# Last layer's adapter gathered for each sequence, value loads one sequence further ahead, first cache gathers moved to rounds 16 to 26, second key turn placed ahead of the values

## The chip, the cores and the metric

The kernel runs on one core of one Trainium2 chip. The metric is the device time of the whole program in microseconds (us), as the median of three runs. In the profile PE is the matmul engine, PEld its weight loads, DVE the vector engine, ACT the scalar engine, POOL the GpSimd engine, SP the engine that only issues transfers.

## The reference

There are 64 sequences of 64 tokens with 512 channels. Four layers follow one another, each added to its input; everything is float32.

```python
x = x + einsum('bct,bcd->bdt', x, weights[cond])                    # layer 0
x = x + x @ W_base.T + (((x @ Wt.T) @ A[i].T) @ B_w[i].T) @ Wp.T * sc[i]   # layer 1
# layer 2: 8 query heads, 4 key/value heads of 64; new keys and values are written into a
# paged cache (257 blocks of 16 tokens a sequence), window of 256 positions, softmax, Wo
x = x + attention(x, caches, block_tables, kv_lens)
# layer 3: one of 8 adapters of rank 16 for each sequence
x = x + x @ W.T + ((x @ A[i].T) @ Bm[i].T) * s[i]
```

## The kernel before

The order of all work is written out by hand: the code runs under a manual schedule, so each engine executes its instructions in the order in which the Python code records them. Transfers are issued on three queues: SP's, ACT's and POOL's. POOL's are the indirect gathers and scatters (helpers `gather`, line 63, recorded at L65, and `scatter`, L71). An engine that waits holds up everything behind it on that engine.

**Rounds.** The first part is a loop of 39 rounds (L882). Rounds 0 to 31 each treat one tile of 128 tokens, which is two sequences: layers 0 and 1 (`first_parts`), the new keys and values (`product_kv`, `new_rows`), and their scatter into two small tables in DRAM, `pk` and `pv` (`put_rows`, L831). All scatters to one table follow each other: each waits until the one before has landed. The queries of a tile come 11 tiles later (`product_q`, `norm_q`, `turn_q`), and their multiplication by the inverse norm is on POOL (L248). Rounds 32 to 38 hold queries alone. At round 32 the last scatters are issued, and behind them on POOL `k_patch(0)`, `v_patch(0)` and `v_patch(1)` (L896 to L898), which gather the patched rows for the first sequences. The first gathers from the old cache are at the rounds that L938 to L949 name: `k_load(0)` at 19 and 20, `v_load(0)` and `v_load(1)` at 21 and 23, `k_copy(0)` at 24 to 27, `v_copy` at 25 and 27, `v_load(2)` at 28, `k_load(1)` at 29 and 30.

**Steps.** The second part is a loop of 128 steps (L1117). A step `s` treats one sequence `b` and one pair of key/value heads `gp`; eight steps make a group `q` of four sequences, and `i = s % 8`. In one step PE computes, in this order: `scores(s + 1)` (tile `psc`), the turn of the probabilities `turn_p(s)` (`pp`), the first turn of keys for the next group (`k_turn`, tile `psk`, steps 3 to 7 by the table `turns`, L1114), one of eight parts of the last layers of the group before (`last_parts`), `values(s)` (`po`), and the second turn of keys. DVE and ACT carry the softmax between: `maxima` (L999), `exponentials` (L1009), `shares` (L1016, L1017), `keep_p` (L1032). Both turns of keys write the single bank `psK`, so a turn waits until the copies of the turn before (L183, L184; on ACT for even `o4`, on DVE for odd) have emptied it; `scores` of a new group wait for the copies of the last turn.

**Values.** For each sequence POOL gathers four times 92 rows (`v_load`, into two buffers `vs_mem`), ACT copies them (`v_copy`, L197, into four buffers `vt_mem`), POOL gathers the patched rows over them (`v_patch`), and three transfers on SP's queue spread 28 of the rows (`v_share`, L208). In the pair of steps of sequence `b` the kernel issues `v_load(b + 3)`, `v_copy(b + 2)`, `v_patch(b + 2)` and `v_share(b + 1)`. Keys go the same way once a group: `k_load` (two gathers), `k_copy` (four copies), `k_patch`, then eight turns.

**The last layers.** `last_parts(q)` (L1051) gives eight parts. The first four multiply by `Wo` (`pso`, L1059). The fifth computes the ranks for all eight adapters at once: `a3_sb` holds 8 x 16 = 128 rows, four matmuls of 128 output rows by 256 columns (`psxa`, L1067), and the product with `mask3` (L1070) leaves each sequence its own adapter, scaled. Then come eight matmuls of 512 columns for `x @ W.T` (`psy`, L1078 and L1084) and two with `bm_sb` (L1086). `mask3` is made in round 19 by `adapters` (L438), the two adapter matrices are loaded in round 9 on ACT's queue (L406, L407).

Of the kernel before, what the change touches and what calls it, by code (L numbers as in the profile page):

```python
# [10 lines left out]
F32 = mybir.dt.float32  # L11
I32 = mybir.dt.int32
AF = mybir.ActivationFunctionType
ALU = mybir.AluOpType
# [4 lines left out]
P = 128  # L19
# [31 lines left out]
def kernel(  # L51
# [41 lines left out]
    def ctile(shape, dt, name, pool=const):  # L93
        return pool.tile(shape, dt, name=name, tag=name)
# [16 lines left out]
    a3_sb = ctile([P, KC, P], F32, "a3_sb")  # L111
    bm_sb = ctile([P, D], F32, "bm_sb")
    iod = ctile([P, 3, 4, 28], F32, "iod")
    ion = ctile([P, 3, 4, 28], F32, "ion")
    mask3 = ctile([P, B], F32, "mask3")
    cen = ctile([P, B], F32, "cen")
    edge = ctile([P, 1], F32, "edge")
    lowb = ctile([P, B], F32, "lowb")
# [175 lines left out]
    with ExitStack() as one:  # L294
# [104 lines left out]
        def late_inputs(part):  # L399
            h = slice(part % 2 * 2, part % 2 * 2 + 2)  # L400
            if part < 2:
                S.dma_start(out=woT_sb[:, h], in_=woT[:, h])
            elif part < 4:
                S.dma_start(out=w3_sb[:, h], in_=w3T.rearrange("(c p) o -> p c o", p=P)[:, h])
            else:
                S.dma_start(out=a3_sb, in_=a3T.rearrange("(c p) r -> p c r", p=P))  # L406
                S.dma_start(out=bm_sb, in_=bm3)  # L407

        def positions(part):

# [12 lines left out]
        def rows0():  # L423

            make_identity(nc, ident)
            iota(pcol, [[0, 1]], 0, 1)
            for _, hs in halves():
                iota(tcol[hs], [[0, 1]], 0, 1)
            for bd in bds:
                G.memset(bd, 0.0)  # L430
            condf = t1([P, B], F32, "condf")
            V.tensor_copy(condf, cond_i)
            for h, hs in halves():
                V.tensor_scalar(
                    cidx[hs], condf[hs].rearrange("p (n two) -> p n two", two=2)[:, :, h],
                    float(T), tcol[hs], ALU.mult, ALU.add)

        def adapters(ad_i, scb, e, dst):  # L438

# [442 lines left out]
        for n in range(NLAST):  # L882
            if n % 4 == 0:
                parts = first_parts(n // 4 + 1)
            w_load0(n + 12)
            x2_load(queries(n + 2))
            if 1 <= n <= NTILE:
                new_rows(n - 1)
            if n != NTILE:
                norm_q(queries(n - 1))()  # L890
            lag = 4 if n < 20 else 3 if n < 22 else 2 if n < 24 else 1
            while done["p"] <= min(n - lag, NTILE - 1):
                put_rows(done["p"])
                done["p"] += 1
            if n == NTILE:
                k_patch(0)  # L896
                v_patch(0)
                v_patch(1)  # L898
                norm_q(queries(n - 1))()
            product_q(queries(n), psP)  # L900
            if n % 4:
                x_load0(n + 8)
            if n in (14, 16, 18, 20):
                gather_indices((n - 14) // 2)
            if n < NTILE:
                parts[n % 4]()
            if n % 4 == 0:
                x_load0(n + 8)
            if n == 1:
                written_rows()  # L910
                places()
            if n in (1, 2):
                for o4 in (0, 1):
                    fill_copy(2 * (n - 1) + o4)
            if n == 2:
                fill_store(pv)
            if n >= 2:
# [7 lines left out]
            if 5 <= n < 10:  # L925
                late_inputs(n - 5)
            if 14 <= n < 18:
                positions(n - 14)
            if n == 19:
                adapters(ad3_i, sc3b, 8, mask3)  # L930
                middles()
            if n == 21:
                residual3()
                G.memset(sm_mem, 0.0)
            turn_q(queries(n - 5 if n == NTILE else n - 2 if n != NTILE - 3 else -1), psO)
            if n < NTILE:
                product_kv(n)
# [12 lines left out]


    def pool2(name, bufs):
# [98 lines left out]
    def last_parts(q):  # L1051

        psy, xa, xq, oT = {}, {}, xqs.pop(q), oTs.pop(q)

        def out_product(ec):
            ps = bank(psM, f"pso{q}_{ec}")
            o = ps[:, :256].rearrange("p (b t) -> p b t", t=T)
            for c in range(4):
                PE.matmul(o, lhsT=woT_sb[:, c, ec * P : (ec + 1) * P],  # L1059
                          rhs=oT[:, c // 2, :, c % 2, :],  # L1060
                          start=(c == 0), stop=(c == 3))
            V.tensor_tensor(xq[:, ec], ps[:, :256], xq[:, ec], ALU.add)

        def ranks():
            ps = bank(psM, f"psxa{q}")
            for c in range(KC):
                PE.matmul(ps[:, :256], lhsT=a3_sb[:, c, :], rhs=xq[:, c],  # L1067
                          start=(c == 0), stop=(c == KC - 1))
            xa[0] = mp.tile([P, 4, T], F32, name=f"xa{q}", tag="xa")
            V.tensor_tensor(  # L1070
                xa[0], ps[:, :256].rearrange("p (b t) -> p b t", t=T),
                mask3[:, 4 * q : 4 * q + 4].unsqueeze(2).to_broadcast([P, 4, T]), ALU.mult)

        def y_first(i):
            n = 2 * q + i
            psy[i] = bank(psM, f"psy{n}")
            for c in range(2):
                PE.matmul(psy[i], lhsT=xq[:, c, i * P : (i + 1) * P], rhs=w3_sb[:, c, :],  # L1078
                          start=(c == 0), stop=False)

        def y_rest(i):
            n = 2 * q + i
            for c in range(2, KC):
                PE.matmul(psy[i], lhsT=xq[:, c, i * P : (i + 1) * P], rhs=w3_sb[:, c, :],  # L1084
                          start=False, stop=False)
            PE.matmul(psy[i], lhsT=xa[0].rearrange("p b t -> p (b t)")[:, i * P : (i + 1) * P],  # L1086
                      rhs=bm_sb, start=False, stop=True)
# [29 lines left out]
    for s, (q, b, gp) in enumerate(steps):  # L1117
# [15 lines left out]
        scores(s + 1)  # L1133
        turn_p(s)
        if 0 < s < 16:
# [13 lines left out]
        second()  # L1149
        if gp:  # L1150
            window(b + 2)
        po = values(s)
        if turn2:
            k_turn(q + 1, *turn2)
        keep_o(s, po)
        if gp == 0:
            v_copy(b + 2)
        if i == 0:
            k_copy(q + 1, 3)
        elif i > 4:  # L1160
            k_copy(q + 2, i - 5)
        if i == 7:
            parts += last_parts(q)
    for part in parts:
# [52 lines left out]
```

## Time and profile before

| what | us |
|---|---|
| median of 3 runs (lowest to highest) | 1236.24 (1232.07 to 1236.6) |
| the profiled execution's own time | 1225.52 |
| its span in the trace | 1223.7 |
| POOL, old values: gathers `vs_mem`, 256 | 310.2 |
| POOL, patched values: gathers `vt_mem`, 64 | 80.0 |
| POOL, old keys: gathers `kt`, 32 | 30.6 |
| PE, `pso`, `psxa`, `psy` with `bm_sb` | 123.2, 30.8, 32.7 |

The program starts 1225.52 - 1223.7 = 1.8 us before or after what the trace spans; the rest of the text counts in the trace's time. The fp32 matmuls each leave two rows in the trace, so 64 matmuls of `psxa` are 128 rows. Busy times are unions: where matmuls overlap, the mean length of one is more than its share. "Idle before" names the time in which an engine stood still just ahead of a group, and what ended it. The page cuts the span into 40 slices: the rounds fill slices 1 to 15, steps begin near 480 us, and the last slice is the tail after the last step. Over slices 20 to 39 the busy share of DVE, ACT and POOL is 5 to 7 tenths each, and PE stands at 8 or 9 tenths.

### The profile page before, as it was taken

How to read it: one execution, taken by the hardware profiler on the slowest of the kernel's cores; microseconds unless marked ns; L12 is line 12 of the kernel's file. 1: busy time of each engine (PE TensorE's matmuls, PEld its weight loads, DVE VectorE, ACT ScalarE, POOL GpSimd, SP SyncE). 2: the span in 40 equal slices, each digit the busy share in tenths (PEclk: the TensorE clock that was granted, in tenths of full speed). 3: DMA queues.
4: the chain of work that ended last, by engine and by line, in shares of the span. 5: the costliest groups of instructions: out<-in, count | busy, mean ns of one | idle time of the engine just before them, and what ended most of it. 6: DMA issues, size and time to landing. Idle time of an engine off the chain costs nothing.

```text
span 1223.7 us, 17686 instructions
## 1 busy us (share of the span) xinstructions
PE 1107.0 (90%) x5622; PEld 639.8 (52%) x5622; DVE 753.0 (62%) x2313; ACT 571.2 (47%) x1472; POOL 613.9 (50%) x601
## 2 busy tenths in 40 slices
PE   4998899999999968879989989999999899999998
PEld 4434444444444434446656656555655565665665
DVE  3775346766666755875665655665665665666561
ACT  1332222232233324555655655655665565666651
POOL 3243323332543351887566666656656656656620
PEclk9999899999899988998999999999999999999999
DMA  8375713234331363546546556556555745756420
GB/s 270 123 258 209 241 41 113 74 102 131 111 114 51 108 171 111 157 117 147 129 113 161 130 126 143 147 126 142 147 127 140 167 121 121 161 139 150 99 64 35
DMA packets 129820, 163.20 MB, mean 133 GB/s; under 512 B 58079, under 2 KB 96891, under 8 KB 125545
## 3 DMA queue, kind: packets, MB, share of 16 engines
q0 software_dynamic: 63872, 85.04, 28.5%
q1 hardware_dynamic: 46416, 53.89, 14.5%
q10 hardware_dynamic: 19440, 23.15, 5.6%
q8 instruction: 45, 0.74, 0.3%
q14 instruction: 47, 0.39, 0.1%
HBM read 139.66 MB, written 50.33 MB: 155 GB/s over the span
## 4 chain that ended last, share of the span: by engine, by line
PE 66%; DVE 8%; issue 7%; DMA 6%; POOL 6%; ACT 3%; ACTq 0%; POOLq 0%; DVEq 0%; SPq 0%
PE pso L1059 9%; PE pp L1025 8%; PE po L1041 7%; PE psc L983 7%; PE ps L787 5%; PE psy L1084 5%; PE q L263 5%; PE kv L820 5%; PE psk L175 4%; PE psy L1078 4%; PE psxa L1067 2%; PE psy L1086 2%; DMA pv<-vt_mem,zidx 2%; POOL vs_mem L65 2%; PE ps L789 2%
## 5 line engine op out<-in xcount | busy, mean ns | idle before, releaser
L65 POOL DMA_INDIRECT vs_mem<-in_vblk_dram,iv_old x256 | 310.2, 1212 | 77.4 <-issue 70.5
L1009 ACT ACTIVATE sm_mem<-sm_mem,mn 128x336 f32<-128x336 f32 x256 | 145.6, 574 | 32.5 <-DVE mn L999 26.9
L65 POOL DMA_INDIRECT vt_mem<-pv,iv_new x64 | 80.0, 1250 | 160.2 <-ACT vt_mem L197 84.0
L999 DVE CUSTOM_DVE_ANT_0 sm_mem<-psc,pen 128x336 f32<-128x336 f32 x256 | 119.6, 501 | 43.6 <-PE pp L1025 22.8
L1041 PEld LDWEIGHTS po<-pT,vt_mem 124*64 124x64 f32 x1536 | 84.9, 137 | 87.0 <-ACT sm_mem L1009 49.2
L1041 PE MATMUL po<-pT,vt_mem 124*64 124x128 f32 x1536 | 118.4, 282 | 12.5 <-ACT pT L1032 7.3
L1059 PE MATMUL pso<-oT,woT_sb 128*128 128x256 f32 x512 | 123.2, 385 | 0.0
L263 PE MATMUL q<-wq_sb,x2q 128*128 128x512 f32 x256 | 120.8, 617 | 1.9 <-DMA x2q<-x2d 1.9
L1025 PE MATMUL pp<-ident,sm_mem 128*124 128x128 f32 x768 | 115.5, 283 | 6.8 <-issue 2.9
L1025 PEld LDWEIGHTS pp<-ident,sm_mem 128*124 128x124 f32 x768 | 81.3, 139 | 70.7 <-issue 58.6
L983 PE MATMUL psc<-kT_mem,qs 64*128 64x336 f32 x512 | 108.2, 498 | 10.7 <-DVE kT_mem L184 9.9
L787 PE MATMUL ps<-kT_mem,kT_mem 128*128 128x512 f32 x256 | 116.9, 600 | 0.6 <-PE ps_fill L493 0.6
L820 PE MATMUL kv<-wkv_sb,xr 128*128 128x512 f32 x256 | 115.4, 595 | 0.4 <-ACT va L828 0.4
L1017 DVE TENSOR_SCALAR sm_mem<-sm_mem,rsum 128x336 f32<-128x336 f32 x256 | 107.2, 419 | 9.1
L248 POOL TENSOR_TENSOR q<-q,rsq 128x512 f32<-128x512 f32 x30 | 31.5, 1050 | 139.7 <-DVE rsq L246 109.0
L1059 PEld LDWEIGHTS pso<-oT,woT_sb 128*128 128x128 f32 x512 | 92.5, 192 | 12.6 <-ACT pen L973 2.1
L175 PE MATMUL psk<-ident,k 84*128 84x84 f32 x512 | 63.8, 251 | 22.9 <-ACT kT_mem L184 9.1
L263 PEld LDWEIGHTS q<-wq_sb,x2q 128*128 128x128 f32 x256 | 50.0, 200 | 61.4 <-issue 61.2
L787 PEld LDWEIGHTS ps<-kT_mem,kT_mem 128*128 128x128 f32 x256 | 49.0, 193 | 61.5 <-issue 60.3
L1032 DVE COPY pT<-pp 124x384 f32<-124x384 f32 x128 | 70.8, 553 | 16.4 <-PE pp L1025 6.9
L1032 ACT COPY pT<-pp 124x384 f32<-124x384 f32 x128 | 61.6, 482 | 35.5 <-PE pp L1025 25.0
L820 PEld LDWEIGHTS kv<-wkv_sb,xr 128*128 128x128 f32 x256 | 46.9, 190 | 57.0 <-issue 55.5
(223 smaller groups left out, 1748.5 us busy)
## 6 DMA issues: line engine op xcount, KB each, us to landing
xt<-in_x_dram SPq DMA_DIRECT2D x32, 256.0 KB
x2d<-xr SPq DMA_DIRECT2D x8, 1024.0 KB
x2q<-x2d SPq DMA_DIRECT2D x32, 256.0 KB
qd<-qt ACTq DMA_DIRECT2D x64, 128.0 KB
qs<-qd SPq DMA_DIRECT2D x16, 512.0 KB
xq<-x2d SPq DMA_DIRECT2D x16, 512.0 KB
out_dram<-ys ACTq DMA_DIRECT2D x32, 256.0 KB
vt_mem<-vt_mem SPq DMA_DIRECT2D x192, 28.0 KB
```

Source lines behind the costliest of these rows:

```text
L65: G.indirect_dma_start(out=dst, out_offset=None, in_=src, in_offset=bass.IndirectOffsetOnAxis(ap=idx, axis=0), **more,)
L175: PE.transpose(ps[:, oq, :], k2[:NP, 4 * oq + o4, 2 * gp : 2 * gp + 2].rearrange("p g d -> p (g d)"), ident[:NP, :NP])
L263: PE.matmul(psq[n], lhsT=xt[:, c, :], rhs=wq_sb[:, c, :], start=(c == 0), stop=(c == KC - 1))
L787: PE.matmul(ps, lhsT=wb_sb[:, c, oc * P : (oc + 1) * P], rhs=x1_mem[:, c, :], start=(c == 0), stop=False)
L820: PE.matmul(pskv[n], lhsT=xrs[s][:, c, i * P : (i + 1) * P], rhs=wkv_sb[:, c, :], start=(c == 0), stop=(c == KC - 1))
L983: PE.matmul(pscs[s][g], lhsT=qts[q][gs, gp, b % 4].rearrange("p h t -> p (h t)"), rhs=kT(q, gp)[gs, b % 4].rearrange("p o c i -> p (o c i) ...
L999: V.tensor_tensor_reduce(rows4(sm)[:, :, :, :28], rows4(pscs[s][g]), rows4(pens[b]), SCALE, 3.0e38, ALU.add, ALU.min, mn)
L1009: S.activation(w, w, AF.Exp, bias=mn, scale=-1.0, accum_out=rsum)
L1025: PE.transpose(pp[:NVK, o, :], sms[s][g][0][:, o * P : o * P + NVK], ident)
L1032: (V.tensor_copy if g else S.copy)(pT, pps[s][g][:NVK])
L1041: PE.matmul(po[g * HD : (g + 1) * HD, :], lhsT=vt(b)[:NVK, o, 2 * gp + g], rhs=pTs[s][g][:, o, :], start=(o == 0), stop=(o == 2))
L1059: PE.matmul(o, lhsT=woT_sb[:, c, ec * P : (ec + 1) * P], rhs=oT[:, c // 2, :, c % 2, :], start=(c == 0), stop=(c == 3))
```

## The change

The rank matrix of the last layer is no longer computed for all adapters. Two new tables, `ia3` and `ib3`, name for each sequence the rows of its adapter; `a_load` gathers for one sequence a [128, 16 x 4] piece of A (the DRAM copy is laid out anew for that), `b_load` for four sequences the rows of B. That is five gathers a group on POOL. With them `ranks` has eight matmuls of 32 output rows by 128 columns, at four column places of the array, and the product with B has two matmuls of 64 contraction rows. The four terms of a rank lie on two strips that B's gathered rows repeat. The order of the last four parts changes with it.

The value pipeline is one sequence longer (`v_load(b + 4)`, `v_copy(b + 3)`, `v_patch(b + 3)`), `v_share(b + 1)` and `k_patch` come one step earlier, the last `k_copy` of a group moves from step 0 to step 7 of the group before, the second key turn goes ahead of `values`, and the first gathers move to rounds 16 to 26. The two loads of round 9 are gone. `adapters` is called for layer 1 alone.

```diff
+        def last_adapters():
+            adf = t1([P, B], F32, "adf8")
+            V.tensor_copy(adf, ad3_i)
+            V.tensor_scalar(ia3, adf, float(P), pcol, ALU.mult, ALU.add)
...
+            for e in range(1, 8):
+                V.tensor_scalar(part, adf, float(e), sc3b[:, e : e + 1], ALU.is_equal, ALU.mult)
+                V.tensor_tensor(scl, scl, part, ALU.add)
...
+            V.tensor_reduce(idx, pick, AX.X, ALU.add)
+            V.tensor_scalar(ib3, idx, 16.0, r_f, ALU.mult, ALU.add)
...
                 v_patch(1)
+                v_patch(2)
...
-                adapters(ad3_i, sc3b, 8, mask3)
+                last_adapters()
...
-            if n in (NTILE - 13, NTILE - 12):
-                k_load(0, n - (NTILE - 13))
-            if n in (NTILE - 11, NTILE - 9):
-                v_load((n - (NTILE - 11)) // 2)
-            if n in (NTILE - 7, NTILE - 5):
-                v_copy((n - (NTILE - 7)) // 2)
-            if NTILE - 8 <= n < NTILE - 4:
-                k_copy(0, n - (NTILE - 8))
-            if n in (NTILE - 3, NTILE - 2):
-                k_load(1, n - (NTILE - 3))
-            if n == NTILE - 4:
-                v_load(2)
+            if n in (NTILE - 16, NTILE - 15):
+                k_load(0, n - (NTILE - 16))
+            if n in (NTILE - 12, NTILE - 11, NTILE - 7, NTILE - 6):
+                v_load(n - (NTILE - 12) if n < NTILE - 10 else n - (NTILE - 9))
+            if n in (NTILE - 9, NTILE - 8, NTILE - 4):
+                v_copy(min(n - (NTILE - 9), 2))
+            if NTILE - 13 <= n < NTILE - 9:
+                k_copy(0, n - (NTILE - 13))
+            if n in (NTILE - 9, NTILE - 8):
+                k_load(1, n - (NTILE - 9))
...
         def ranks():
-            ps = bank(psM, f"psxa{q}")
+            ps = bank(psM, f"psxa{q}")[:, :P]
             for c in range(KC):
-                PE.matmul(ps[:, :256], lhsT=a3_sb[:, c, :], rhs=xq[:, c],
-                          start=(c == 0), stop=(c == KC - 1))
+                for i in range(2):
+                    lo = i * 64 + c % 2 * 32
+                    PE.matmul(ps[lo : lo + 32, :],
+                              lhsT=a3_mem[:, 2 * i : 2 * i + 2, :, c].rearrange("p b r -> p (b r)"),
+                              rhs=xq[:, c, i * P : (i + 1) * P], start=(c < 2), stop=(c >= 2))
...
+        def y_ranks():
+            for i, hs in halves():
+                PE.matmul(psy[i], lhsT=xa[0][hs].rearrange("p b t -> p (b t)"), rhs=b3_mem[hs],
+                          start=False, stop=False)
...
-            lambda: (ranks(), y_first(0)), lambda: y_rest(0), lambda: y_first(1), lambda: y_rest(1)]
+            lambda: (ranks(), y_base(0, (0,), start=True)),
+            lambda: (y_base(1, (0,), start=True), y_ranks()),
+            lambda: (y_base(0, (1, 2, 3), stop=True), y_store(0)),
+            lambda: (y_base(1, (1, 2, 3), stop=True), y_store(1))]
+    def a_load(q, i):
+        gather(a3_mem[:, i].rearrange("p r c -> p (r c)"), a3T, ia3[:, 4 * q + i : 4 * q + i + 1])
+    def b_load(q):
+        gather(b3_mem, bm3, ib3[:, q : q + 1])
...
-    for o4 in range(3):
+    for o4 in range(4):
         k_copy(1, o4)
...
+        if i == 0:
+            k_patch(q + 1)
         if gp == 0:
-            v_load(b + 3)
+            v_share(b + 1)
+            v_load(b + 4)
         else:
-            v_share(b + 1)
-            v_patch(b + 2)
-        if i == 1:
-            k_patch(q + 1)
+            v_patch(b + 3)
...
+        if i in (5, 6):
+            a_load(q, 2 * (i - 5))
+            a_load(q, 2 * (i - 5) + 1)
+        if i == 7:
+            b_load(q)
...
-        po = values(s)
         if turn2:
             k_turn(q + 1, *turn2)
+        po = values(s)
         keep_o(s, po)
         if gp == 0:
-            v_copy(b + 2)
-        if i == 0:
-            k_copy(q + 1, 3)
-        elif i > 4:
+            v_copy(b + 3)
+        if i > 4:
             k_copy(q + 2, i - 5)
+        if i == 7:
+            k_copy(q + 2, 3)
```

More of the change, by code (lines that the diff above doesn't have):

```diff
@@ L110 @@
     w3_sb = ctile([P, KC, D], F32, "w3_sb")
-    a3_sb = ctile([P, KC, P], F32, "a3_sb")
-    bm_sb = ctile([P, D], F32, "bm_sb")
+    a3_mem = ctile([P, 4, 16, KC], F32, "a3_mem")
+    b3_mem = ctile([P, D], F32, "b3_mem")
     iod = ctile([P, 3, 4, 28], F32, "iod")
     ion = ctile([P, 3, 4, 28], F32, "ion")
-    mask3 = ctile([P, B], F32, "mask3")
+    mask3 = ctile([P, B // 4, 2], F32, "mask3")
+    ia3 = ctile([P, B], I32, "ia3")
+    ib3 = ctile([P, B // 4], I32, "ib3")
     cen = ctile([P, B], F32, "cen")
@@ L404, in late_inputs @@
                 S.dma_start(out=w3_sb[:, h], in_=w3T.rearrange("(c p) o -> p c o", p=P)[:, h])
-            else:
-                S.dma_start(out=a3_sb, in_=a3T.rearrange("(c p) r -> p c r", p=P))
-                S.dma_start(out=bm_sb, in_=bm3)
         def positions(part):
@@ L436, in rows0 @@
                     float(T), tcol[hs], ALU.mult, ALU.add)
+        def last_adapters():
+            adf = t1([P, B], F32, "adf8")
+            V.tensor_copy(adf, ad3_i)
+            V.tensor_scalar(ia3, adf, float(P), pcol, ALU.mult, ALU.add)
+            seq_i, r_i = t1([P, 1], I32, "seq_i"), t1([P, 1], I32, "r_i")
+            own_s, r_f = t1([P, 2], F32, "own_s"), t1([P, 1], F32, "r_f")
+            V.tensor_copy(seq_i, pcol)
+            V.tensor_scalar(r_i, seq_i, 15, None, ALU.bitwise_and)
+            V.tensor_copy(r_f, r_i)
+            V.tensor_scalar(seq_i, seq_i, 4, 1, ALU.arith_shift_right, ALU.bitwise_and)
+            V.tensor_copy(own_s[:, 1:], seq_i)
+            V.tensor_scalar(own_s[:, :1], own_s[:, 1:], -1.0, 1.0, ALU.mult, ALU.add)
+            scl, part = t1([P, B], F32, "scl8"), t1([P, B], F32, "part8")
+            V.tensor_scalar(scl, adf, 0.0, sc3b[:, :1], ALU.is_equal, ALU.mult)
+            for e in range(1, 8):
+                V.tensor_scalar(part, adf, float(e), sc3b[:, e : e + 1], ALU.is_equal, ALU.mult)
+                V.tensor_tensor(scl, scl, part, ALU.add)
+            pick = part[:, : B // 2].rearrange("p (q s) -> p q s", s=2)
+            for h, hs in halves():
+                own_b = own_s[hs].unsqueeze(1).to_broadcast([HD, B // 4, 2])
+                two = slice(2 * h, 2 * h + 2)
+                V.tensor_tensor(mask3[hs], scl[hs].rearrange("p (q i) -> p q i", i=4)[:, :, two],
+                                own_b, ALU.mult)
+                V.tensor_tensor(pick[hs], adf[hs].rearrange("p (q i) -> p q i", i=4)[:, :, two],
+                                own_b, ALU.mult)
+            idx = scl[:, : B // 4]
+            V.tensor_reduce(idx, pick, AX.X, ALU.add)
+            V.tensor_scalar(ib3, idx, 16.0, r_f, ALU.mult, ALU.add)
         def adapters(ad_i, scb, e, dst):
@@ L924 @@
                 mixers(n // 4 + 2)
-            if 5 <= n < 10:
+            if 5 <= n < 9:
                 late_inputs(n - 5)
@@ L1064, in ranks, with y_base, y_store @@
         def ranks():
-            ps = bank(psM, f"psxa{q}")
+            ps = bank(psM, f"psxa{q}")[:, :P]
             for c in range(KC):
-                PE.matmul(ps[:, :256], lhsT=a3_sb[:, c, :], rhs=xq[:, c],
-                          start=(c == 0), stop=(c == KC - 1))
-            xa[0] = mp.tile([P, 4, T], F32, name=f"xa{q}", tag="xa")
+                for i in range(2):
[3 more added lines that the diff above has]
+                              rhs=xq[:, c, i * P : (i + 1) * P], start=(c < 2), stop=(c >= 2))
+            xa[0] = mp.tile([P, 2, T], F32, name=f"xa{q}", tag="xa")
             V.tensor_tensor(
-                xa[0], ps[:, :256].rearrange("p (b t) -> p b t", t=T),
-                mask3[:, 4 * q : 4 * q + 4].unsqueeze(2).to_broadcast([P, 4, T]), ALU.mult)
-        def y_first(i):
+                xa[0], ps.rearrange("p (b t) -> p b t", t=T),
+                mask3[:, q].unsqueeze(2).to_broadcast([P, 2, T]), ALU.mult)
+        def y_base(i, cs, start=False, stop=False):
             n = 2 * q + i
-            psy[i] = bank(psM, f"psy{n}")
-            for c in range(2):
+            if start:
+                psy[i] = bank(psM, f"psy{n}")
+            for c in cs:
                 PE.matmul(psy[i], lhsT=xq[:, c, i * P : (i + 1) * P], rhs=w3_sb[:, c, :],
-                          start=(c == 0), stop=False)
-        def y_rest(i):
-            n = 2 * q + i
[L1083 to L1087, printed above, removed]
+                          start=start and c == cs[0], stop=stop and c == cs[-1])
+        def y_ranks():
+            for i, hs in halves():
+                PE.matmul(psy[i], lhsT=xa[0][hs].rearrange("p b t -> p (b t)"), rhs=b3_mem[hs],
+                          start=False, stop=False)
+        def y_store(i):
+            n = 2 * q + i
             ys = ap2.tile([P, D], F32, name=f"ys{n}", tag="ys")
@@ L1199 @@
         "w3T": a["L3_cond_W"].T,
-        "a3T": a["L3_cond_A"].reshape(P, D).T,
+        "a3T": a["L3_cond_A"].reshape(8, 16, KC, P).transpose(0, 3, 1, 2).reshape(8 * P, 64),
         "bm3": a["L3_cond_Bm"].transpose(0, 2, 1).reshape(P, D),
```

## The prediction, made before the result

> **What bounds the kernel now.** I read the page's busy shares first, then the chain of work that ended last, then PE's waits in the stretch between two rank products of the chain, then POOL's rows of one period.
>
> ```profile
> span 1223.7 us, 17686 instructions
> PE 1107.0 (90%) x5622; PEld 639.8 (52%) x5622; DVE 753.0 (62%) x2313; ACT 571.2 (47%) x1472; POOL 613.9 (50%) x601
> ```
>
> PE is busy for 90% of the span and nothing else is near it; the chain also lies on PE for 66%. The chain's rows give the length of one group of eight steps:
>
> ```profile
> 620.77 1.76 PE psxa L1067 x8
> ...
> 1144.94 1.77 PE psxa L1067 x8
> ```
>
> The rank product comes once a group. The two rows stand twelve groups apart: (1144.94 - 620.77) / 12 = **43.68 us a period**. The view of windows and PE's waits over exactly this stretch:
>
> ```profile
> 620.77:1144.94 524.17, 486.67 (x3218) 310.43 (x3217) 327.24 (x1104) 318.65 (x852) 325.85 (x276) 1.00 0.58 138
> ```
> ```profile
> PE psc L983 <- DVE kT_mem L184: 8.2, 12, 0.9
> PE psk L175 <- issue: 6.1, 13, 0.9
> PE psk L175 <- PE pp L1025: 5.9, 4, 1.6
> PE psk L175 <- ACT kT_mem L184: 5.5, 6, 1.8
> PE po L1041 <- issue: 4.9, 10, 0.7
> PE po L1041 <- ACT pT L1032: 3.3, 3, 1.2
> ```
>
> The window's first column after the length is PE's busy time, 486.67 / 12 = 40.56 a period, so PE stands still for 3.1. The waits (total, times, longest) say where: before the key turns (`psk`, 6.1 + 5.9 + 5.5 + 0.3 = 17.8, or 1.48 a period), before a new group's scores (`psc`, 0.68 a period), before the values (`po`, 0.68). POOL, the fifth busy column, works 325.85 / 12 = 27.15 a period in 23 gathers, but it cannot issue them back to back:
>
> ```profile
> 564.70 1.22 POOL L65 DMA_INDIRECT vs_mem<-in_vblk_dram,iv_old  x1 [0.30 <-issue]
> 566.22 1.20 POOL L65 DMA_INDIRECT vs_mem<-in_vblk_dram,iv_old  x1 [0.30 <-PE pp L1025]
> ```
>
> Each has 0.30 ahead of it, so POOL's own period is 27.15 + 23 x 0.30 = **34.05**, with 9.6 of slack.
>
> **The change part by part, per period.**
>
> *Ranks.* Removed: four matmuls of 128 output rows by 256 columns, 1.76 (the chain row). Added: eight of 32 output rows by 128 columns. The nearest row is `po` (64 output rows, 128 columns), 12 rows or six matmuls in 0.81 from start to next start (724.14 to 724.94, listed length 0.88): 0.135 each, 8 x 0.135 = 1.08. Gain 0.68. Bounds: 0.54 if strips run twice as much abreast as `po`'s, and 1.76 if a matmul of half the columns costs half of 0.44 and nothing overlaps.
>
> *Product with B.* Removed: two matmuls of 128 rows by 512, 0.86 each, 1.72. Added: two of 64 contraction rows on two halves of the array; nearest is `psc`, two matmuls of 64 rows by 336 in 0.77 (719.85 to 720.62), times 512 / 336 = 1.17. Gain 0.55; bounds 0.86 (fully abreast) and 1.72. Together 1.23, bounds 0 to 2.1.
>
> The rows put a `po` and a `psc` next to full products with no listed gap (690.50 `po`, 691.40 `psc`, 692.16 `pp`). The Trainium skill speaks against the change here: "TensorEngine Tiling (Array Packing)", section Key Properties, says that a change of tiling mode drains the array, and the change adds four such switches a period. With some 128 cycles for a drain, from "TensorE: Matmul & The Clock Gate", section Step-by-step: what each phase is for, an estimate would be 0.2 a period and a median of 1198 rather than the forecast; no row of this trace prices a drain.
>
> *Second key turn ahead of the values.* Its copies get the time of `values` (0.81) before the next user of the bank. The wait of `psc` (0.68, longest 0.9) goes; of the 1.48 before the turns the one of step 6 goes (0.45 at 721.94) and about a third of the rest, together 0.8; a turn (0.44) placed ahead of `po` fills 0.3 of its 0.68. Sum 1.8; bounds 0, since the softmax's loop through DVE and ACT may simply hand the waits to `pp` and `po`, and 2.6 (psc and psk whole, with 0.4 of po). What is late next is `po` on `pT`. PE alone would have 43.68 - 1.23 - 1.8 = 40.65.
>
> *POOL.* Five gathers come in. `a_load` has 128 rows of 256 B, as have the adapter gathers of the rounds:
>
> ```profile
> L65 POOL DMA_INDIRECT wg<-in_w_dram,cidx x32 | 31.8, 992 | 38.1 <-DVE bd L754 27.4 <-issue 5.9 <-DVE cidx L434 3.4
> ```
>
> 5 x (0.99 + 0.30) = 6.45; bounds 5 x 1.25 (`kt`, 0.95) and 5 x 1.55 (`vt_mem`, 1.25): 6.3 to 7.8. POOL's own period becomes **40.5**, as long as PE's. POOL also waits: `v_patch` for ACT's copy or the shares (129.1 / 48 = 2.7 each time, 10.8 a period). These waits are mostly its slack, and shrink when it is late; the extra sequence of lead makes the copy come earlier. A late POOL is felt through ACT, which waits in `v_copy` for `vs_mem` to land, with the probabilities' copies behind it. What is queued behind `a_load` is the next `v_load`; a_load itself waits for the ranks of step 4, which are over before step 5.
>
> Two loops of 40.65 and 40.5 that wait on each other do not both run free. I take back 0.75 of the 1.8, and take **41.4**, bounds 40.5 (POOL's sum) and 43.7. Fourteen periods: 14 x 2.3 = **-32**. Group 15 and the tail have no key turns and few gathers: 2 x 1.23, **-2**.
>
> *End of the rounds.* Here PE's longest wait but one stands, and POOL is its cause:
>
> ```profile
> 435.80 0.99 POOL L65 DMA_INDIRECT kt<-in_kblk_dram,ik_old  x1 [0.31 <-issue]
> 440.63 1.00 POOL L71 DMA_INDIRECT pv<-va,sidx  x1 [3.85 <-DMA pk<-k,sidx]
> ...
> 447.15 0.97 POOL L71 DMA_INDIRECT pv<-va,sidx  x1 [4.22 <-DMA pv<-va,sidx]
> ...
> 452.48 1.03 POOL L65 DMA_INDIRECT k<-pk,ik_new  x1 [3.08 <-DMA pk<-k,sidx]
> ```
> ```profile
> 457.79 1.12 PE L283 MATMUL pst<-ident,q 128*128 128x128 f32 x4 [9.65 <-POOL q L248]
> ```
>
> Four `vs_mem` gathers (422.91 to 428.81) and two `kt` gathers stand between scatters that must land one after another; the patches end at 456.65, and only then comes the multiplication L248 for which PE waits 9.65. With the gathers out of these rounds the scatters keep the pace of rounds without gathers, 3.2 (308.64 to 311.80). The `pv` scatter that goes at 429.12 now can go near 423.5 (the gathers ahead of it take 6.2), three more end its chain at 433.5, the last `pk` lands some 4 after that, near 438.8, and `k_patch` (1.33) and three `v_patch` (one more than before, 1.55 each) end near 444.8; DVE's `rsq` is ready at 443.1. `pst` follows 1.1 after the start of L248, as now, near 446 instead of 457.79: **-11**. Bounds -8 (scatters no faster than 4) and -13.5 (wait 9.65, the 1.87 on `x2q`, and two products at 3.60 instead of 4.62).
>
> *First group, 486 to 548.* POOL is busy 54.05 of 62 there, with the last queries' inverse norms (1.83 + 1.04) between gathers. Five gathers more, 6.45, of which 3.0 is found idle in its steps 5 to 7; `k_patch(1)` now waits for the fourth key copy, near 491.3 where POOL is free at 489.6, +1.6. Less the gain of one early `v_patch`: **+4**, bounds 0 and +8.
>
> *Costed at nothing.* `last_adapters` has 23 more DVE instructions in round 19; DVE is 31.5 busy of the 50 in 250 to 300. Uncovered they cost 23 x 0.2 = 4.6. The fourth `k_copy` (ACT, 1.04) moves from step 0 to 7: ACT is 26.6 busy of 43.7. The moved gathers lie where POOL waits for `rsq` (109.0 in all, 5 to 12 a round); if they push an L248 out they cost PE what they overrun, 1.5 each. `v_share` a step earlier holds SP's queue, with the loads of `xq` and `qs` behind it; SP already waits 375.1 there (57 times, longest 12.9) with PE not waiting for either load. Two loads of 512 KB leave ACT's queue in round 9, where PE's waits are not on them.
>
> Sum: -32 - 2 - 11 + 4 = **-41**. The profiled execution took 1225.52, and the median of the runs is 1236.24, 10.7 above; the differences are worked out in the former and set off from the latter: 1236.2 - 41 = **1195**.
>
> **The rivals.**
> 1. *POOL is no hindrance.* The waits that shrink are all its slack and PE keeps the whole 3.0: period 40.6, 14 x 3.1 = 43; 1236.2 - 43 - 2 - 7 = **1184**. For: the 2.7 before each `vt_mem` is long and ended by ACT, not by data. Against: no slack is left, and each loop that slips then moves the other.
> 2. *POOL binds with some waits on top.* 40.5 + 1.9 (a fifth of 10.8) = 42.4; -18 - 2 - 7: **1209**. For: `v_patch` waits on the landing of other transfers (20.9 of 160.2) that no lead shortens.
> 3. *The waits come back in the softmax, and small tiles do not run abreast.* The period falls by 0.5: -7 - 2 - 7: **1220**, or 1230 to 1242 if the first group costs 8 and the period does not fall. For: PE's `po` waits already end on `pT`. Against: PE had no wait of that kind in 1060 to 1145, where a period is 42.
> 4. *POOL falls behind: slower.* The place is `v_patch(b + 3)` behind the added `a_load` in steps 5 to 7. It decides when the five gathers cost more than (43.68 - 34.05) / 5 = 1.93 each, or bring 3.2 us of new waits a period; then ACT stands in `v_copy` and PE behind it. At a period of 45: +18 - 2 - 7, **1246**. For: a wait inside POOL's queue holds all later gathers. Against: the nearest rows cost 1.25 to 1.55.
>
> That the change does not do what it says is little of a rival: the recorded order on PE does put the second turn before `values`, and five gathers a group are there.
>
> **How the numbers follow.** Forecast (41 to 42) 0.38; rival 1 0.17; rival 2 0.23; rival 3 0.10; rival 4 0.12. The range goes from 1174 (a period at POOL's 40.5, 14 x 3.2 = 44.5, 2 x 2.1 for group 15 and the tail, 13.5 at the end of the rounds, nothing lost in the first group) to 1224 (rival 3); out of it fall half of rival 3, rival 4 and a little below, 0.2. About 0.5%, 6 us, is what can be told from no change: faster is the first three and half of the fourth, 0.83; same is the other half and 0.02 of rival 4, 0.07; slower 0.10.
>
> **What would show it.** Right: `psxa` near 1.1 and the B product near 1.2; no wait of `psc` on `kT_mem`; rank products 41.4 apart; POOL's gathers `a3_mem` x64 and `b3_mem` x16 near 1.0; no wait of 9.65 at `pst` near 446 to 458. Wrong: `vt_mem` or `vs_mem` waits on PE's chain, `v_copy` on ACT waiting for landings, `pp` or `po` waits up by what `psk` lost, or new waits of PE in rounds 16 to 26.

## The result, and the profile after

The changed kernel takes 1311.8 us in the median of four runs (1302.41 to 1327.09), against 1236.42 (1232.07 to 1244.99) for the kernel before in the same series: a ratio of **1.0575, interval 1.0486 to 1.0665**. The forecast was 1195, and the range ended at 1224. The experiments below add something that one number hides: on another chip, where the kernel before takes 1199.9, the ratio of the same two kernels is 0.9993 (0.9957 to 1.0030).

The page of the changed kernel, its first part:

```profile
span 1310.9 us, 18171 instructions
PE 1119.8 (85%) x5750; PEld 637.1 (49%) x5750; DVE 765.6 (58%) x2335; ACT 568.1 (43%) x1472; POOL 693.6 (53%) x680
```

PE has more busy time than before (1119.8 against 1107.0), although its work became less, and a smaller share. The next two rows are rank products thirteen groups apart; the window between them has the columns of the windows shown in the prediction.

```profile
579.05 1.08 PE L1099 MATMUL psxa<-xq,a_mem 128*32 128x128 f32 x11
...
1234.62 0.67 PE L1099 MATMUL psxa<-xq,a_mem 128*32 128x128 f32 x16
```
```profile
579.05:1234.62 655.57, 545.64 (x3589) 339.09 (x3588) 363.63 (x1201) 342.63 (x924) 418.12 (x363) 0.95 0.50 128
```

A period is 655.57 / 13 = 50.43 us where it was 43.68. PE is busy for 41.97 of it (before 40.56) and idle for 8.46 (before 3.1). Thirteen times 6.75 is 88, and the spans differ by 87.2: what comes before and after them about cancels out, and the loss lies in these groups. It has two parts, idle time (+5.4 a period) and matmuls that last longer (+1.4, though the new tiles save some).

**Results are seen late.** PE's waits of this window, and then one stretch of it on three engines:

```profile
PE po L1071 <- issue: 21.8, 34, 4.0
PE po L1071 <- ACT pT L1062: 12.9, 16, 5.8
PE po L1071 <- DVE pT L1062: 12.6, 9, 3.4
PE psk L177 <- ACT kT_mem L186: 11.8, 12, 4.2
```
```profile
710.50 0.83 PE L1013 MATMUL psc<-kT_mem,qs 64*128 64x336 f32 x4
713.06 1.02 PE L1055 MATMUL pp<-ident,sm_mem 128*124 128x128 f32 x6 [1.73 <-PE psc L1013]
713.92 1.89 PE L1089 MATMUL pso<-oT,woT_sb 128*128 128x256 f32 x8
721.57 1.62 PE L1071 MATMUL po<-pT,vt_mem 124*64 124x128 f32 x12 [5.76 <-ACT pT L1062]
```
```profile
713.33 0.56 DVE L1002 SCALAR_TENSOR_TENSOR pen<-ion,lowb,pen 128x336 f32<-128x336 f32 x1
717.80 0.51 DVE L1029 CUSTOM_DVE_ANT_0 sm_mem<-psc,pen 128x336 f32<-128x336 f32 x1 [3.91 <-remote]
```
```profile
717.76 0.27 ACT L1079 COPY oT<-po 128x128 f32<-128x128 f32 x1 [3.25 <-remote]
721.04 0.48 ACT L1062 COPY pT<-pp 124x384 f32<-124x384 f32 x1 [3.02 <-remote]
```

The scores (`psc`) end by the model at 711.33, and DVE, idle since 713.89, begins to read them at 717.80. ACT begins to copy `po`, which was issued at 709.70, at 717.76, and `pp`, which ended by the model at 714.08, at 721.04. Both engines stand still, both are let go within 0.04 us, and then `po` waits 5.76 for ACT. The readers were not slow: the trace records the updates of PE's semaphore at 717.73 and 717.78, 0.02 to 0.03 ahead of both starts. What PE had produced was signalled, and seen, 6 to 7 us after its modelled end. On the other chip the scores of the next step of the same kernel read:

```profile
690.01 0.84 PE L1013 MATMUL psc<-kT_mem,qs 64*128 64x336 f32 x4
```
```profile
690.87 0.51 DVE L1029 CUSTOM_DVE_ANT_0 sm_mem<-psc,pen 128x336 f32<-128x336 f32 x1
```

Modelled end 690.85, semaphore update 690.85, start 690.87; DVE was busy until then. The Trainium skill, "Perfetto Trace Analysis", section Tensor Engine Instruction, says that a matmul's end is computed and that its semaphore is sent only once PSUM has acknowledged the bytes. By that, rows alone cannot tell a late matmul from a late signal: model and start differ by at most 0.02 here on one chip and by 6.5 on another, and which of the two is late no run shows.

**The clock follows.** PE stands from 715.81 to 721.57, and the seventh column of figures in the windows is the granted clock:

```profile
716.00:720.00 4.00, 0.00 (x0) 0.00 (x0) 1.03 (x4) 0.27 (x1) 3.32 (x3) 0.75 0.34 86
720.00:724.00 4.00, 2.43 (x16) 1.73 (x16) 1.97 (x6) 2.34 (x7) 0.00 (x0) 0.50 0.63 180
```

After the wait the clock is 0.50, and the scores at 723.12 take 1.49 instead of 0.83. Over the execution the clock was 0.953 against 0.976 before. The traces' clock records hold 1 and 0.5 alone, so that is 2 x 0.047 x 1310.9 = 123 us at half speed against 59. In the window of thirteen groups it is 70.7 us, in the prediction's window of the kernel before none. PE is busy in 59.2 of the 70.7, so an estimate of what half speed costs is 59.2 / 2 / 13 = 2.3 a period, most of the 1.4 added and the 1.8 that the small tiles save. The Trainium skill, "TensorE: Matmul & The Clock Gate", section What's actually happening, says the same: an idle window of some 3.4 us brings half the clock.

### The profile page after: what moved, and what is told of

Same layout as the page of the kernel before. It is cut to its first block, busy times and chain, and to the rows that moved or that the text cites. A ratio compares the mean times of both kernels' runs of the same rounds, so it can differ in the third digit from the quotient of the medians.

```text
span 1310.9 us, 18171 instructions
## 1 busy us (share of the span) xinstructions
PE 1119.8 (85%) x5750; PEld 637.1 (49%) x5750; DVE 765.6 (58%) x2335; ACT 568.1 (43%) x1472; POOL 693.6 (53%) x680
## 4 chain that ended last, share of the span: by engine, by line
PE 55%; DVE 12%; issue 10%; ACT 7%; POOL 6%; DMA 3%; another core or an unknown queue 3%; ACTq 0%; POOLq 0%; SPq 0%; DVEq 0%
PE po L1071 7%; PE pso L1089 7%; PE ps L818 6%; PE pp L1055 6%; PE kv L851 6%; PE psc L1013 5%; PE q L265 5%; PE psy L1112 5%; PE psk L177 3%; POOL vs_mem L65 3%; PE ps L820 2%; DVE sm_mem L1047 2%; PE psz L803 1%; ACT k L159 1%
## 5 line engine op out<-in xcount | busy, mean ns | idle before, releaser
L1071 PE MATMUL po<-pT,vt_mem 124*64 124x128 f32 x1536 | 133.6, 293 | 54.7 <-issue 24.1
L1029 DVE CUSTOM_DVE_ANT_0 sm_mem<-psc,pen 128x336 f32<-128x336 f32 x256 | 121.7, 503 | 77.6 <-PE pp L1055 34.7
L1055 PE MATMUL pp<-ident,sm_mem 128*124 128x128 f32 x768 | 121.9, 289 | 27.9 <-DVE rsum L1046 7.9
L1071 PEld LDWEIGHTS po<-pT,vt_mem 124*64 124x64 f32 x1536 | 93.4, 142 | 103.2 <-issue 48.6
L1013 PE MATMUL psc<-kT_mem,qs 64*128 64x336 f32 x512 | 114.3, 523 | 18.0 <-DVE kT_mem L186 11.0
L1112 PE MATMUL psy<-w_sb,xq 128*128 128x512 f32 x256 | 127.7, 623 | 0.8 <-issue 0.8
L1089 PE MATMUL pso<-oT,woT_sb 128*128 128x256 f32 x512 | 127.5, 393 | 0.7 <-ACT oT L1079 0.6
L1047 DVE TENSOR_SCALAR sm_mem<-sm_mem,rsum 128x336 f32<-128x336 f32 x256 | 111.3, 435 | 9.0
L1079 ACT COPY oT<-po 128x128 f32<-128x128 f32 x128 | 33.6, 263 | 121.3 <-PE pp L1055 52.8
L177 PEld LDWEIGHTS psk<-ident,k 84*128 84x128 f32 x512 | 52.5, 151 | 65.5 <-issue 33.4
```

The lines of the kernel that those rows point to most:

```text
L177: PE.transpose(ps[:, oq, :], k2[:NP, 4 * oq + o4, 2 * gp : 2 * gp + 2].rearrange("p g d -> p (g d)"), ident[:NP, :NP])
L1013: PE.matmul(pscs[s][g], lhsT=qts[q][gs, gp, b % 4].rearrange("p h t -> p (h t)"), rhs=kT(q, gp)[gs, b % 4].rearrange("p o c i -> p (o c i) ...
L1047: V.tensor_scalar(w, w, rsum, None, ALU.mult)
L1055: PE.transpose(pp[:NVK, o, :], sms[s][g][0][:, o * P : o * P + NVK], ident)
L1071: PE.matmul(po[g * HD : (g + 1) * HD, :], lhsT=vt(b)[:NVK, o, 2 * gp + g], rhs=pTs[s][g][:, o, :], start=(o == 0), stop=(o == 2))
L1089: PE.matmul(o, lhsT=woT_sb[:, c, ec * P : (ec + 1) * P], rhs=oT[:, c // 2, :, c % 2, :], start=(c == 0), stop=(c == 3))
```

## The experiments

For every run the table has the ratio to the kernel before in its own series (intervals in brackets), the period (mean of thirteen, between rank products) and a **delay**. For the delay I paired every maxima L1029 (L999 before) with the scores that it reads, and every L1092 with its `pso`, kept those ahead of which DVE stood idle, after 560 us, and took the start minus the modelled end.

| run | kernel before | ratio | period | mean delay (number over 1 us, of) |
|---|---|---|---|---|
| before, first profile | 1236.4 | | 43.7 | 1.06 (38 of 96) |
| after, first profile | 1236.4 | 1.0575 [1.0486, 1.0665] | 50.4 | 2.13 (87 of 126) |
| c_before | 1233.7 | 1.0018 [0.9979, 1.0056] | 44.4 | 1.21 (44 of 101) |
| c_after | 1233.7 | 1.0486 [1.0415, 1.0557] | 48.6 | 1.88 (109 of 148) |
| e5_group0_adapters | 1233.7 | 1.0249 [1.0152, 1.0345] | 46.9 | 2.16 (101 of 124) |
| e6_old_last_turns | 1233.7 | 1.0439 [1.0348, 1.0529] | 48.5 | 2.03 (99 of 131) |
| h0_group0_adapters | 1238.9 | 1.0151 [1.0089, 1.0213] | 47.0 | 2.12 (111 of 131) |
| h1_no_key_gathers | 1238.9 | 1.0030 [1.0000, 1.0060] | 44.1 | 0.81 (26 of 103) |
| h2_no_value_patches | 1238.9 | 1.0166 [1.0086, 1.0246] | 47.6 | 2.20 (77 of 112) |
| h3_before_no_keys | 1238.9 | 0.9654 [0.9597, 0.9710] | 41.5 | 0.17 (1 of 71) |
| e1_old_last | 1198.6 | 0.9856 [0.9816, 0.9897] | 41.1 | 0.06 (0 of 53) |
| e2_old_turns | 1198.6 | 1.0095 [1.0061, 1.0129] | 42.9 | 0.11 (0 of 61) |
| e3_kpatch_back | 1198.6 | 1.0094 [1.0060, 1.0129] | 43.0 | 0.19 (0 of 81) |
| e4_vpipe_back | 1198.6 | 1.0136 [1.0087, 1.0186] | 43.0 | 0.15 (0 of 72) |
| g0_old_last | 1199.9 | 0.9857 [0.9783, 0.9932] | 41.1 | 0.06 (0 of 53) |
| g1_pipe_only | 1199.9 | 0.9928 [0.9893, 0.9963] | 42.4 | 0.16 (0 of 81) |
| g2_kpatch_only (profile of its longest run) | 1199.9 | 1.0108 [1.0008, 1.0207] | 44.0 | 0.09 (0 of 57) |
| g3_after | 1199.9 | 0.9993 [0.9957, 1.0030] | 42.0 | 0.10 (0 of 60) |
| i1_pipe_only | 1199.4 | 0.9917 [0.9886, 0.9949] | 41.8 | 0.15 (0 of 83) |
| i2_kpatch_only | 1199.4 | 1.0135 [1.0089, 1.0182] | 43.7 | 0.06 (0 of 53) |

By the run records, the series with 1198.6 and 1199.9 ran on chip 1, the one with 1199.4 on chip 8, the one with 1233.7 on chip 5 and the one with 1238.9 on chip 10; for the first comparison no chip is recorded. I call 1 and 8 the quick chips and the others, with that of the first comparison, the slow ones, after the kernel before. Only chip 1 was used in two series, so something else that differs between series, such as where the data lay, is not excluded as the source.

### First series: undo one part at a time (quick chip)

`e1_old_last` takes back `ranks`, the parts of `last_parts`, `adapters` and the loads of round 9; `e2_old_turns` the order of two calls; `e3_kpatch_back` the place of the key patch; `e4_vpipe_back` the pipeline. The copies, loads and patches ahead of the steps that belong to the last two go back as well and are left out here:

```diff
 e2_old_turns
-        if turn2:
-            k_turn(q + 1, *turn2)
         po = values(s)
+        if turn2:
+            k_turn(q + 1, *turn2)
 e3_kpatch_back
-        if i == 0:
-            k_patch(q + 1)
...
             v_patch(b + 3)
+        if i == 1:
+            k_patch(q + 1)
...
+        if i == 0:
+            k_copy(q + 1, 3)
-        if i == 7:
-            k_copy(q + 2, 3)
 e4_vpipe_back
-            v_share(b + 1)
-            v_load(b + 4)
+            v_load(b + 3)
         else:
-            v_patch(b + 3)
+            v_share(b + 1)
+            v_patch(b + 2)
...
-            v_copy(b + 3)
+            v_copy(b + 2)
```

> The changed kernel with the last layers of the kernel before (rank product for all adapters, no gathers of adapters). Theory A, POOL's five added gathers are what costs: about 1230, 80 below the changed kernel. Theory B, key patch at the head of step 0 (62 us of new waits at the head of POOL's queue): no more than 15 below, about 1300. Theory C, second key turn ahead of the values: about 1310. Theory D, the transfers of the longer value pipeline meet those of keys and of the x and q loads: about 1305.

> The changed kernel with the values ahead of the second key turn again. Theory C: about 1235, 75 below the changed kernel. Theories A, B and D: within 15 of 1312.

> The changed kernel with the key patch behind the value patch of step 1 and the fourth key copy in step 0, as before the change. Theory B: about 1240, with the 62 us of waits of the key patch gone from POOL's list. Theory D: some 20 to 40 below 1312, as one part of the traffic moves by a step. Theories A and C: within 15 of 1312.

> The changed kernel with the value pipeline as long as before (loads three ahead, copies and patches two ahead, shares with odd steps). Theory D: about 1240. Theories A, B and C: within 15 of 1312.

The numbers of all four expectations missed: the kernel before itself took 1198.6 here, and the changed kernel had not been run beside them. No theory follows from this series alone; read with `g3_after` (0.9993 on the same chip, another series) it says that each of turns, key patch and pipeline is worth 1.0 to 1.4% to the changed kernel there, and the new last layers cost 1.4%.

### Second series: the changed kernel and the one before, again (slow chip)

> The changed kernel again, beside the others of this series. The kernel before took 1198.6 in the first series of experiments, not 1236. If the chip has no part in the loss: 1.0575 times the kernel before, some 1268. If the loss needs a chip on which the results of the matmuls are seen late (the kernel before at 1236): at most 1.015 times the kernel before.

> The kernel before, for its profile beside the others. Where it takes about 1199: periods of about 42 instead of 43.7, and no starts of DVE and ACT that come 1 to 2 us after the modelled end of the matmul. Where it takes 1236: as in the first profile.

`e5_group0_adapters` gathers for the first group only; `e6_old_last_turns` is `e1_old_last` with the two calls of `e2_old_turns`:

```diff
-        if i in (5, 6):
+        if s in (5, 6):
             a_load(q, 2 * (i - 5))
             a_load(q, 2 * (i - 5) + 1)
-        if i == 7:
+        if s == 7:
             b_load(q)
```

> The changed kernel with adapters gathered for the first group alone; the other groups use the same ones, so that the last layer is that of other adapters from the second group on. 75 of 80 gathers of adapters are left out, the small matmuls stay. Theory A (the five gathers a group are what costs): below the version with the old last layers by 14 to 16 periods of 1.7, so 0.965 of the kernel before. Theory B (key patch at the head of step 0): as the changed kernel.

> The version with the old last layers, and the values ahead of the second key turn again: what is left is the longer value pipeline, the order of POOL and the early gathers. If the second turn ahead of the values is worth 1.8 a period: 25 above the version with the old last layers, 1.007 of the kernel before. If it is worth nothing: as that version, 0.986.

The loss came back on a chip where the kernel before takes 1233.7. Theories A (adapters) and C (turns) fall as its whole cause: `e6_old_last_turns` has neither and still takes 1.0439, with a delay as large as the changed kernel's; both numbers expected for it missed. `e5_group0_adapters` (1.0249) lies between what A and B expected: leaving the adapters' gathers out is worth 0.024 of the 0.049. What is left in `e6_old_last_turns` is the longer value pipeline, the key patch in step 0 and the early gathers.

### Third series: the remaining two parts (quick chip 1 again)

`g1_pipe_only` is `e6_old_last_turns` with the edit of `e3_kpatch_back`, `g2_kpatch_only` with that of `e4_vpipe_back`.

> The version with the old last layers again, whose ratio was 0.986 where the kernel before took 1199. If a chip on which results are seen late turns gains into losses: where the kernel before takes 1230 or more, at or above 1.02; where it takes 1199, 0.986 again.

> Of the change in the steps only the longer value pipeline with the shares a step earlier (key patch behind the value patch of step 1, old turns, old last layers; early gathers as changed). Theory B (key patch at the head of step 0 costs): at most 1.00 of the kernel before, where the version with both was 1.044. Theory D (longer pipeline costs): 1.03 or more there.

> Of the change in the steps only the key patch at the head of step 0 and the fourth key copy in step 7 (value pipeline, turns and last layers as before; early gathers as changed). Theory B: 1.03 or more where the kernel before takes 1230. Theory D: at most 1.00.

> The changed kernel once more. If the loss needs a chip on which results are seen late: at most 1.015 where the kernel before takes 1199, 1.05 where it takes 1230 or more. If the chip has no part in it: 1.05 on either.

This chip shows no delay, in any kernel, and the changed kernel loses nothing, as expected for it. What `g0`, `g1` and `g2` were to tell of a slow chip stays unanswered. The series does show what the changed kernel is bound by when results come in time. POOL first, then PE's and ACT's longest waits, from one rank product to the one thirteen groups on:

```profile
573.01:1119.14 546.13, 505.09 (x3589) 325.92 (x3589) 364.76 (x1196) 341.57 (x923) 423.17 (x367) 0.98 0.69 155
```
```profile
PE po L1071 <- ACT pT L1062: 30.7, 26, 3.0
```
```profile
ACT vt_mem L199 <- DMA vs_mem<-in_vblk_dram,iv_old: 49.7, 12, 5.6
```

POOL works 423.17 / 13 = 32.55 a period in 28 gathers; with 0.30 ahead of each that is 40.95 of 42.01. PE needs only 505.09 / 13 = 38.85. So POOL, with 1.06 to spare, is the nearest bound; ACT stands in `v_copy` until the value rows land, and PE's `po` waits for the probabilities queued behind that copy. Without the new last layers (`g0_old_last`) POOL has slack and PE goes from rank product to rank product in 41.12:

```profile
567.41 1.93 PE L1066 MATMUL psxa<-xq,a_sb 128*128 128x256 f32 x8
...
1102.01 1.93 PE L1066 MATMUL psxa<-xq,a_sb 128*128 128x256 f32 x8
```

It was faster than both kernels on this chip, twice (0.9856 and 0.9857); on a slow chip it was not run.

### Fourth series: which transfers delay the results (slow chip)

`h1_no_key_gathers` and `h3_before_no_keys` have the same edit, on the changed kernel and on the one before; `h2_no_value_patches` patches eight sequences:

```diff
 h1_no_key_gathers, h3_before_no_keys (k_load and k_patch)
-        if q < B // 4:
+        if q < 2:
             gather(...)
 h2_no_value_patches
-        if b < B:
+        if b < 8:
             gather(vt_mem[:NV, b % 4], ...)
```

> The changed kernel with adapters gathered for the first group alone (from the second group on the last layer uses the first group's adapters). Where the kernel before takes 1199 and the changed kernel the same: the small matmuls are worth 14 x 1.6 and POOL has its slack back, so 0.97. If the small matmuls gain nothing: 0.986, as the version with the old last layers.

> The changed kernel without the gathers of old and new keys from the third group on (keys of the groups before are used again). If the packets of 8 and 16 KB that these gathers move make the matmuls' results reach DVE and ACT late where the kernel before takes 1230 or more: the late starts in steps 3 to 5 go, and with them the loss, to 0.96 of the kernel before. If the lateness has another source: no more than the 3 gathers of POOL a group, 1.03. Where the kernel before takes 1199: 0.97, for POOL's 3 x 1.3 a group.

> The changed kernel without the value patches from the ninth sequence on (new values are left out there). POOL has 4 x 1.55 a group less, as if four of the five adapter gathers had gone, and waits for ACT's copies no more. If small packets of the patches make results late: the loss goes. If the keys' packets do: 1.01 to 1.03 where the kernel before takes 1230. Where it takes 1199: 0.965, if POOL's length is what holds the changed kernel there.

> The kernel before without the gathers of keys from the third group on. If these packets make results late in it too: 0.96 where it takes 1236, and 0.99 or more where it takes 1199, as POOL has slack in it.

In the kernel before, leaving out three gathers a group takes the delay from 1.1 or 1.2 to 0.17 and the period to an even 41.5, with a ratio of 0.9654 (0.96 was expected). The window of thirteen groups, and PE's waits in it:

```profile
570.24:1110.13 539.89, 519.72 (x3487) 334.84 (x3485) 356.21 (x1195) 344.64 (x923) 313.90 (x261) 1.00 0.37 99
```
```profile
PE psc L983 <- DVE kT_mem L184: 8.6, 13, 0.7
PE psk L175 <- issue: 7.6, 17, 0.6
PE psk L175 <- ACT kT_mem L184: 3.8, 9, 0.5
```

POOL had 9.6 a period to spare there, and the delay is what changed, so I put the gain down to it: **some 2 us of the 43.7 in the very profile that the prediction was worked out from**. That is argued, as the edit also takes work from POOL; that the same kernel with all its gathers takes 34 to 40 us less on the quick chips points the same way, but it was not profiled there. The changed kernel itself was not run on this chip; set against its other slow series (delay 2.13 and 1.88), the same edit takes its ratio to 1.003 and the delay to 0.81, where 0.96 or 1.03 was expected. 

What remains in `h1_no_key_gathers` sits elsewhere. The trace records the updates of PE's semaphore. I counted, from 560 us to step 118, the matmuls that update it and call one late when no update follows within 0.06 us of its modelled end; in the changed kernel the packets of the key gathers (8 and 16 KB) lie in steps 1 to 4 of a group:

| run | late in steps 1 to 4 | late in the other steps |
|---|---|---|
| before, first profile | 214 of 406 | 93 of 375 |
| h3_before_no_keys | 110 of 394 | 64 of 375 |
| after, first profile | 316 of 416 | 215 of 362 |
| h1_no_key_gathers | 139 of 418 | 263 of 362 |
| g3_after (quick) | 4 of 416 | 1 of 362 |

Without key gathers the lateness falls in the steps where they ran; in the changed kernel it stays in the others, step 6 among them (94 of 98 in the first profile, 72 of 98 in `h1_no_key_gathers`). So the key gathers are not its only source there, and no run tells what else is. Value patches seem to have a part in the time (1.0166 without them, in the range of 1.01 to 1.03 that was expected if the keys' packets do it) and none in the delay (2.20), so their small packets are not the source. `h0_group0_adapters` keeps a delay of 2.12 with hardly any adapter gathered, so these gathers are not its source either; their part in the time (1.0151 and 1.0249 without them, 1.0486 and 1.0575 with) I put down to POOL's queue. The delay alone does not order the runs: `h0_group0_adapters` has 2.12 at 1.0151, `e6_old_last_turns` 2.03 at 1.0439.

### Fifth series: pipeline or key patch (quick chip 8)

> Again the kernel with only the longer value pipeline and the shares a step earlier (and the early gathers); 0.993 where the kernel before takes 1200. Where it takes 1230 or more: 1.03 or above if the value loads that run further ahead meet the key transfers and the x and q loads there and make more results late; 1.00 or below if the key patch in step 0 does.

> Again the kernel with only the key patch at the head of step 0 and the fourth key copy in step 7 (and the early gathers); 1.011 where the kernel before takes 1200. Where it takes 1230 or more: 1.03 or above if the key patch in step 0, beside the x and q loads, makes more results late; 1.00 to 1.01 if the longer pipeline does.

The chip was another one, as quick as the first, so the question was not answered. The ratios repeat those of the third series, near what was expected for such a chip.

## Why the prediction was wrong

**The step that failed** is the reading of the bound: "PE stands still for 3.1. The waits (total, times, longest) say where". It takes PE's work, the order and POOL's sum for all that sets a period, and the sum has no term for results that are seen late. In `h3_before_no_keys`, with the order untouched and the delay nearly gone, PE stands still for (539.89 - 519.72) / 13 = 1.55 a period: the wait of `psc` stays (0.66 against 0.68), that before the turns goes from 1.48 to 0.88, that before `po` (0.68) is no longer listed. So about half of the 3.1 was order and half was not. Two things follow:
- On the quick chip the period of the changed kernel was nearly the forecast one (42.0 against 41.4), but the kernel before takes 1199.9 there instead of 1236.4, and nothing is won.
- On slow chips, with results as late as shown, it was 50.4 and 48.6. With the delay down to 0.81 it was 44.1 (`h1_no_key_gathers`).

The delay is 1.9 to 2.2 in every slow-chip run with the longer value pipeline, the moved key patch and its key gathers, against 1.1 to 1.2 in the kernel before. Why the change makes it longer no run shows; that it packs transfers more closely is a guess.

**Rival 4** had the sign ("POOL falls behind: slower") and neither the mechanism nor the price: POOL's gathers cost what the rows said, and a period was 50.4, not 45. One of its conditions did hold, at a place that I had costed for the first group alone. `k_patch` at the head of step 0 waits for the fourth key copy: it starts 0.30 after the end of that copy in each of these groups (704.13 after 703.83), whatever releaser a row names. POOL's waits in the window of the changed kernel:

```profile
POOL k L65 <- PE pso L1089: 47.1, 11, 7.9
...
POOL k L65 <- DVE pT L1062: 7.3, 1, 7.3
...
POOL k L65 <- ACT k L159: 6.0, 1, 6.0
```

That is 60.4 / 13 = 4.6 a period, where the kernel before shows 0.30 each time. It is not shown to be a loss of its own: POOL's work with 0.30 ahead of each gather is 418.12 / 13 + 28 x 0.30 = 40.6 of the 50.4 here, and on the quick chip the same waits are 8.3 / 13 = 0.6. On the quick chips the key patch alone costs 1.1 and 1.4% (`g2_kpatch_only`, `i2_kpatch_only`), and in the company of the other parts it gains 1.0% (`e3_kpatch_back` is slower without it); what it does on a slow chip was not told apart.

**The other terms, one by one:**
- *Small tiles:* right, and better than forecast. From start to next start the ranks take 0.60 (forecast 1.08) and the product with B 1.06 (1.17), together 1.8 saved where 1.23 was put and 2.1 was the bound. The two rows that show it:

```profile
730.96 0.68 PE L1099 MATMUL psxa<-xq,a_mem 128*32 128x128 f32 x16
731.56 0.70 PE L1112 MATMUL psy<-w_sb,xq 128*128 128x512 f32 x1
```
```profile
737.08 1.13 PE L1118 MATMUL psy<-b_mem,xa 64*128 64x512 f32 x4
738.14 0.51 PE L177 MATMUL psk<-ident,k 84*128 84x84 f32 x4
```

  The switches of tiling, which the prediction priced at an estimated 0.2 a period, show no gap: nothing is listed ahead of the next product. As PE's ends are modelled, a price inside the 0.60 and the 1.06 is not excluded.
- *POOL:* right as a sum, on the chip where nothing else disturbs it: 40.95 against 40.5, and a period of 42.0 against 41.4. There the five gathers cost more than the small tiles win: the last layers as a whole are a loss of 1.4%.
- *Turns:* worth 1% to the changed kernel on the quick chip (1.0095 without), 42.9 - 42.0 = 0.9 a period where 1.8 was put, or 1.05 after the 0.75 taken back.
- *End of the rounds:* the wait of 9.65 is gone, PE is busy 17.85 of 20 in 440 to 460 instead of 8.48, and the first values start at 489.39 instead of 490.76 (483.93 and 491.68 in the second series). Between the matmul below and the first values the changed kernel gains 7.0, and 10.1 in the second series, where 11 was put. Ahead of it 5.0 is lost, for which the prediction had the price (4.6) but costed it at nothing, the 23 added DVE instructions of round 19:

```profile
313.06 2.07 PE L794 MATMUL ps<-bd,xt 128*128 128x128 f32 x8 [7.42 <-ACT kT_mem L796]
```
```profile
307.45 2.07 PE L763 MATMUL ps<-bd,xt 128*128 128x128 f32 x8 [2.38 <-ACT kT_mem L765]
```

  The second row is the kernel before. Without these instructions and with the early gathers the wait is 2.38 too (`g0_old_last`).
- *First group:* +3.7 (489.39 to 579.05 against 490.76 to 576.7), +1.3 in the second series; forecast +4.
- *The clock:* not in the sum at all. Idle stretches of several us cost twice, as PE runs at half speed after them (0.50 after the 5.76 shown).

**What stays open:** what on the slow chips makes results late, beyond the part that goes with the key gathers, and why the quick chips are free of it; and whether the longer pipeline, the key patch in step 0 or the early gathers lengthen the delay.

## What to carry to other kernels

Before waits are costed as order, compare the start of a reader that stood idle with the end of the matmul it reads: where that gap is 1 us instead of 0.04, the wait is not order, and a new order need not win it. Price a new wait in every period, not only in the first, and hold it against the slack of its queue. A loss or a gain of a few per cent seen on one chip is worth a second chip: here the same pair of kernels stood at 1.06 and 1.05 in two series and at 1.00 in a third, on another chip.

## What was not expected of the hardware

The kernel before took 1198.6 to 1199.9 us on two chips and 1233.7 to 1238.9 on others, with the same transfers. On the quick ones an idle DVE read results 0.04 us after the modelled end at the earliest and 0.6 us at the latest; on the others it read them up to 7 us after it in the stretch shown, and PE's semaphore updates came as late. In the kernel before this goes in good part with the key gathers (214 late updates of 406 in steps 1 to 4, 110 of 394 without these gathers); in the changed kernel it lies in nearly all steps.
